# Four graph layers on one core: the scalars' load and copy, and the groups whose degree sums wait for layer 1

## The chip, the core and the metric

The kernel runs on one core of a Trainium2 chip. The metric is the time of one execution in device microseconds (us); the median of three runs of the kernel before is 1097.2 us (1095.84 to 1097.63).

## What is computed

Four graph layers follow each other on x (4096 rows of 64 values) with one dense 4096 x 4096 matrix adj. Each starts from a layer norm with a relu, and adds its result to x:

```python
h = relu(layernorm(x)); x = x + relu((adj @ h) @ W.T + b)                 # layer 0
h = relu(layernorm(x)); x = x + lorentz_attention(h, adj, ...)            # layer 1
h = relu(layernorm(x)); x = x + expmap0(agg(logmap(h), adj / deg) @ W2 + b2)  # layer 2
h = relu(layernorm(x)); x = x + decayed_neighbours(adj != 0) @ (h @ W3) + b3  # layer 3
```

In layer 1, `h` becomes Lorentz vectors hl, q and k; the weights are `adj * sigmoid((2 + 2 q.k) / att_scale + att_bias)`, computed as a sigmoid with a scale `att_a` and a bias `att_b` made of the scalars `att_scale` and `att_bias`, and their sum with hl is normalised. Three more scalars (`scale`, `scale_q`, `scale_k`) enter hl, q and k as exponentials. In layer 2, `deg` is the row sum of adj: it is needed there for the first time, and it is collected while adj passes by in layers 0 and 1.

## The kernel before, in words

**Tiles.** adj is read transposed, four times in all but for half of layer 2. A tile `adj` is 128 partitions x 1024 values (512 KB): two chunks of 128 source rows against 512 target columns. 512 targets are a *block* (`ib`, 0 to 7), two chunks a *group* (`g`, 0 to 15), so a layer has 8 x 16 tiles, each brought by one load on SP's queue (`feed`, line 829). In layers 0 and 1 there are ten tiles of adj (six of pool `adjp`, four of `adj01`): the next load waits until the oldest tile has been used by everyone who needs it.

**Layer 0.** For each tile PE adds two products to a block's sum (`acc<-adj,HA`, `l0_sums`, line 951). Ahead of it stands the layer norm of all x in four parts (`before0`, line 444): DVE takes the mean away, ACT squares, DVE sums, POOL takes the power -0.5, DVE writes `HA`. When a block's 16 groups are summed, a chain follows (`after0`, line 581, then `before1`, line 462): ACT copies the sum to `e`; PE multiplies it with `W0T` and multiplies `dg` with ones to get the degree; DVE adds the bias and writes the block's rows of x; then layer norm, hl, q and k of layer 1 for this *row block*, with DVE, ACT, POOL and PE in turn. At its end stand transposes of q and k on PE and copies to `qT` and `kT` on ACT. Two such chains run at a time.

**Degree sums.** DVE adds the tiles of a block up in `dg` (the first tile is copied, then one addition per tile, then one of the two halves; `degree_sums`, line 925). A tile is not free before both PE and DVE have used it. For each block some groups are left out in layer 0 and added in layer 1 instead, where the same tiles come by again: `FRONT` (line 30) names them for block 0, `LEFT` (3, 7, 11 and 15) for blocks 1 to 6; block 7 leaves none (`group`, line 891).

```python
degree = (g in (LEFT if ib else FRONT) and ib < NB - 1) == (layer == 1)
```

**Layer 1.** `l1` (line 898) is the order of its tiles: block 0's groups 0 to 13, block 1's groups 0 to 13, then groups 14 and 15 of both, then blocks 2 to 7 in order. The first 12 tiles are loaded alternately with the last 12 of layer 0. For blocks 0 and 1 groups are taken in pairs: PE makes the scores (`mm<-qT,kT`, `l1_atts`, line 987), ACT the sigmoids (`sig<-mm`), DVE the products with adj (`sig<-sig,adj`), PE the sums (`acc<-sig,HL`). There is room for the scores of two groups at a time. Group g needs hl and k of row block g // 2, so groups 12 and 13 need row block 6, and pairs are taken strictly in the order of `l1`.

**The scalars.** The five scalars and the biases b0 and b3 are loaded into one row, `line` (seven loads). They stand first in the list `loads`, which `constants` (line 963) issues on ACT's queue from a due time of 18 us on, with the weights W0T, W1T, Wq and Wk behind them. Then PE spreads the row over 128 partitions with one matmul (`tr<-line,ones_row`, due 28 us), and DVE copies the result to `lines`. From it come `es` (ACT), `att_a` and `att_b` (DVE), and the bias in `after0`; the last group of a block in layer 0 is not taken before `lines` is there (line 955).

**What sets the order.** Each piece of work is a generator that yields the engine it needs next and a time from which it may run. `in_turn` (line 758) always takes the piece that can start first, by costs and due times of a small model (`Pace`, line 67), and the instructions are kept in that order on every engine, through one helper (line 139). The profile therefore names line 139 for nearly everything, and work is told apart by its tiles. An engine that waits for its next instruction lets no later one pass.

Of the kernel before, what the change touches and what calls it, by code (L numbers as in the profile page):

```python
# [19 lines left out]
D = 64  # L20
# [6 lines left out]
NG = NC // G  # L27
HALVED = 2
LEFT = (3, 7, 11, 15)
FRONT = (4,5,6,7,)  # L30
LAST = 2
WAIT = 0.6
EARLY = 12
BEHIND = NG - CB // G
# [112 lines left out]
def kernel(ctx: ExitStack, tc: tile.TileContext, a: dict, out: bass.AP):  # L147
# [3 lines left out]
    nc = tc.nc  # L151
    pace = Pace()
    PE, DVE, ACT, POOL = (
        InOrder(tc, e, pace, name)
        for e, name in (
            (nc.tensor, "PE"), (nc.vector, "DVE"), (nc.scalar, "ACT"), (nc.gpsimd, "POOL"),
        )
    )
# [23 lines left out]
    def fetch(t, src, to=loads):  # L182
        to.append(lambda: ACT.dma_start(out=t, in_=src))
# [9 lines left out]
    NS = len(SCALARS)  # L193
    line = const.tile([1, NS + 2 * D], F32, name="line")
    for n, name in enumerate(SCALARS):
        fetch(line[:, n : n + 1], a[name])
    for n, name in enumerate(("b0", "b3")):
        fetch(line[:, NS + n * D : NS + (n + 1) * D], a[name].rearrange("d o -> o d"))
    ones_row = const.tile([1, P], F32, name="ones_row")
    DVE.memset(ones_row, 1.0)  # L200
    lines = const.tile([P, NS + 2 * D], F32, name="lines")
# [58 lines left out]
    def later_constants():  # L260


        def patterns():
            yield "POOL", lambda: 60.0
            for t, one in [(t, 1.0) for t in rbs] + [(t, 0.25) for t in lbs]:
                POOL.memset(t, 0.0)
                for k in (1, 3):
                    POOL.memset(t[:, :, k, 1:2], one)

        def weights_of_ranks():  # L270


            yield "DVE", lambda: 150.0
            near_f = st["rows"].tile([P, P], F32, name="near_f", bufs=1)
            make_lower_triangular(nc, near_f, val=-1.0, diag=False)
            for q in range(4):
                b = slice(q * Q, (q + 1) * Q)
                DVE.tensor_copy(far[b, :], near_f[b, b])
            diag_f = st["rows"].tile([P, P], F32, name="diag_f", bufs=1)
            DVE.tensor_scalar(diag_f, ident, HERE, None, ALU.mult)  # L280
            yield "DVE", lambda: 150.0
            DVE.tensor_add(near_f, near_f, diag_f)
            DVE.tensor_copy(near, near_f)


            yield "DVE", lambda: 150.0
            DVE.memset(pick, 0.0)
            DVE.memset(spread, 0.0)
            for k in range(KH):
                DVE.memset(pick[:, k, k : k + 1], 1.0)  # L290
            for r in range(4):
                yield "DVE", lambda: 150.0
                b = slice(r * Q, (r + 1) * Q)
                for h in range(2):
                    to = spread[b, h, :, h * NC // 2 : (h + 1) * NC // 2]
                    DVE.tensor_copy(
                        to.rearrange("p q (k r) -> p q k r", r=4)[:, :, :, r],
                        ident[b, r * Q : r * Q + KH].unsqueeze(1).to_broadcast([Q, 4, KH]),
                    )

        return patterns(), weights_of_ranks()
# [48 lines left out]
    spare = [0, 1]  # L350

    def bank():
        k = spare.pop(0)
        t = (ps_two if k else ps_tr).tile([P, W], F32, tag=f"tr{k}", name="tr")
        in_use.append((t, k))
        return t

    def emptied(t):
        k = [k for k in in_use if k[0] is t][0]
        in_use.remove(k)  # L360
        spare.append(k[1])
# [219 lines left out]
    def after0(ib, acc, st):  # L581
        e = rows.tile([P, W], F32, tag="e", name="e")
        ACT.copy(e, acc)
        st["acc_free"][ib % 2] = pace.latest
        yield ON_V, lambda: st["dg_done"].get((0, ib))
        dg = st["dg"][0, ib]
        DVE.tensor_add(dg[:, 0, :], dg[:, 0, :], dg[:, 1, :])
        yield TURN

        ps = bank()  # L590
        v, n = ps[:, 0 : CB * D].rearrange("p (c k) -> p c k", k=D), CB * D
        for c in range(CB):
            b = slice(c * P, (c + 1) * P)
            PE.matmul(v[:, c, :], e[:, b], W0T, start=True, stop=True)
            PE.matmul(ps[:, n + c : n + c + 1], dg[:, 0, b], ones_f, start=True, stop=True)
        st["dg_free"][ib % 2] = pace.latest
        yield ON_V
        DVE.tensor_copy(deg[:, cs(ib), :], ps[:, n : n + CB].unsqueeze(2))
        s = rt("h", [P, CB, D])
        DVE.tensor_add(s, v, b0.to_broadcast([P, CB, D]))  # L600
        DVE.scalar_tensor_tensor(
            x[:, cs(ib), :], s, 0.0, x[:, cs(ib), :], ALU.max, ALU.add
        )
        yield ON_V
# [121 lines left out]
    def follow(gen, on=ON_V, evicts=False):  # L726

        tail.append(
            {"gen": gen, "on": on, "at": pace.latest, "slot": None, "evicts": evicts, "need": None}
        )  # L730
# [24 lines left out]
    def latest(*times):  # L755
        return None if None in times else max(times)
# [56 lines left out]
    opened = {}  # L813

    def with_mark(layer, ib, *gens):
        for gen in gens:
            yield from gen
        rows_at[layer, ib] = pace.latest
# [21 lines left out]
    def used(d):  # L840
        d["left"], d["at"] = d["left"] - 1, max(d["at"], pace.latest)

    def ready(t, more=0.0):
        return pace.ready[pace.name(t)] + more

    def arrival(d, more=0.0):
        return ready(d["adj"], more) if "adj" in d else None
# [43 lines left out]
    def group(layer, ib, g):  # L891
        degree = (g in (LEFT if ib else FRONT) and ib < NB - 1) == (layer == 1)
        return {"layer": layer, "ib": ib, "g": g, "degree": degree, "left": 1 + degree, "at": 0.0}
# [1 line left out]


    l0 = [group(0, ib, g) for ib in range(NB) for g in range(NG)]
    l1 = [group(1, ib, g) for ib in range(2) for g in range(BEHIND)]
    l1 += [group(1, ib, g) for ib in range(2) for g in range(BEHIND, NG)]
    l1 += [group(1, ib, g) for ib in range(2, NB) for g in range(NG)]  # L900
    order = l0[: len(l0) - EARLY] + [d for pair in zip(l0[len(l0) - EARLY :], l1) for d in pair]
# [2 lines left out]
    for d in l0 + l1:  # L904
        n = done[d["layer"], d["ib"]] = done.get((d["layer"], d["ib"]), 0) + 1
# [19 lines left out]
    def degree_sums(layer, work):  # L925

        dg = st["dg"]
        for d in work:
            if not d["degree"]:
                continue  # L930
            first = (layer, d["ib"]) not in dg
            yield "DVE", lambda: latest(
                arrival(d, 4.0), st["dg_free"][d["ib"] % 2] if first else 0.0
            )
            if first:
                t = w01.tile([P, G, W], F32, tag="dg", name="dg", bufs=2)
                dg[layer, d["ib"]] = t
                st["dg_free"][d["ib"] % 2] = None
                DVE.tensor_copy(t, d["adj"])
            else:  # L940
                t = dg[layer, d["ib"]]
                DVE.tensor_add(t, t, d["adj"])
            used(d)
            if d is [e for e in work if e["degree"] and e["ib"] == d["ib"]][-1]:
                st["dg_done"][layer, d["ib"]] = pace.latest
# [5 lines left out]
    def l0_sums():  # L951
        for d in l0:
# [6 lines left out]
            if d["last"]:  # L959
                ib = d["ib"]  # L960
                follow(with_mark(1, ib, after0(ib, acc, st), before1(ib, st)), ON_S, evicts=True)

    def constants():
        for k in range(len(loads)):
            yield "ACT", lambda: 18.0 + 0.5 * k
            loads.pop(0)()
        yield "PE", lambda: 28.0 if spare else None
        ps = bank()
        PE.matmul(ps[:, 0 : NS + 2 * D], ones_row, line, start=True, stop=True)
        yield "DVE", lambda: ready(ps)  # L970
        DVE.tensor_copy(lines, ps[:, 0 : NS + 2 * D])
        emptied(ps)
        opened["lines"] = pace.latest
        yield "ACT", lambda: 32.0

        ACT.activation(es, scal[:, 0:3], AF.Exp)

        DVE.reciprocal(att_a, scal[:, 4:5])
        DVE.tensor_scalar(att_a, att_a, 2.0, None, ALU.mult)
        DVE.tensor_add(att_b, att_a, scal[:, 3:4])  # L980
        for k in range(len(later_loads)):
            yield "ACT", lambda: 240.0 + 0.5 * k
            later_loads.pop(0)()
# [543 lines left out]
    def l3_sum():  # L1527
# [33 lines left out]
            (l2_coshs(), 0, once), (l2_clamps_v(), -1, once), (l2_weights2(), 1, lambda d: 2 if d["two"] else 1 if d["first"] else 0),  # L1561
        ),
        l2_clamps(), l2_gathers(), l3_weights(), l3_pass(), l3_masks(), l3_bias(),
        degree_sums(0, l0), degree_sums(1, l1), constants(), *later_constants(),
    ])


# [43 lines left out]
```

## Time and profile before

| what | us |
|---|---|
| median of three runs (lowest, highest) | 1097.2 (1095.84, 1097.63) |
| the profiled execution's own time | 1093.92 |
| its span, first to last instruction | 1092.2 |
| busy: PE, DVE, ACT, POOL | 1038.4, 929.7, 790.0, 260.2 |
| first product of layer 0 / last one | 11.2 / 202.7 |
| chain of layer 0 of blocks 0, 1, 6, 7: first product with W0T | 39.1, 64.4, 169.1, 208.1 |
| q and k of row block 6: transposed on PE | 211.6, 214.1 |
| first 64x512 scores of layer 1 (block 2) | 256.4 |
| mean granted clock of PE | 0.988 of full |

All times are from the span's start. In the views, "x" with a number counts instructions; on PE one matmul of float32 leaves two rows. In brackets behind an instruction stands how long its engine was idle before it and what ended that. In a window's row each engine has its busy time and its instructions; then come PE's granted clock, the busy share of the 16 DMA engines and the GB/s they moved. A row of the timeline has start, duration, engine, operation and tile. Rows of the same kind that follow each other are merged.

### The profile page before, as it was taken

To read this page: it belongs to the slowest core of one execution; us is meant where nothing else is said; L and a number is where in the kernel's file an instruction comes from. 1 tells how busy PE (TensorE), PEld (TensorE's weight loads), DVE (VectorE), ACT (ScalarE), POOL (GpSimd) and SP (SyncE) were. 2 spreads that over 40 slices of the span, in tenths; PEclk is the share of its full clock that TensorE was granted. 3 is DMA by queue.
4 is the path that set the end of the run, shared out by engine and by line. 5 is a ranking of instruction groups with operands and counts; after the bars stand their busy time and mean duration, and the time that the engine had idled before them with its cause. 6 is when DMAs were issued, how large, how long until landed. Compare 5 with 4: busy or idle time off the path is not lost.

```text
span 1092.2 us, 16919 instructions
## 1 busy us (share of the span) xinstructions
PE 1038.4 (95%) x6032; PEld 464.3 (43%) x6032; DVE 929.7 (85%) x1522; ACT 790.0 (72%) x1228; POOL 260.2 (24%) x151
## 2 busy tenths in 40 slices
PE   7989999999999999999999999999999988999998
PEld 3334444333233333354454454444444444454444
DVE  7778999988999999888998999989899999665650
ACT  1144545466777777799989879888798777677776
POOL 3021312110110011243344344334343431000000
PEclk9899999999999999999999999999999999999999
DMA  8999999976687778544553553445536549999950
GB/s 288 405 360 408 398 380 379 310 238 218 208 281 265 240 263 274 171 143 173 181 184 118 179 206 116 174 154 174 174 122 209 191 154 380 376 409 409 410 221 10
DMA packets 76202, 271.77 MB, mean 249 GB/s; under 512 B 9046, under 2 KB 10070, under 8 KB 76118
## 3 DMA queue, kind: packets, MB, share of 16 engines
q1 hardware_dynamic: 75456, 270.57, 68.3%
q8 instruction: 47, 0.77, 0.3%
q14 instruction: 37, 0.30, 0.1%
q10 hardware_dynamic: 662, 0.13, 0.1%
HBM read 269.62 MB, written 1.05 MB: 248 GB/s over the span
## 4 chain that ended last, share of the span: by engine, by line
PE 54%; DVE 21%; issue 8%; ACT 6%; POOL 5%; DMA 4%; SPq 1%; ACTq 0%; DVEq 0%; POOLq 0%
PE acc L139 27%; PE mm L139 17%; PE tr L139 10%; DVE dg L139 5%; POOL v L139 4%; DMA adj<-in_adjT_dram 4%; DVE t L139 4%; DVE w L139 3%; DVE sig L139 3%; ACT sig L139 2%; ACT t L139 1%; ACT lo_sq L139 1%; ACT v L139 1%; DVE h L139 1%; DVE ln_v L139 1%
## 5 line engine op out<-in xcount | busy, mean ns | idle before, releaser
L139 PE MATMUL acc<-w,HA 128*65 128x256 f32 (+1 forms) x736 | 246.2, 470 | 8.6 <-DVE w L139 8.4
L139 POOL TENSOR_SCALAR v<-v 128x1024 f32<-128x1024 f32 (+1 forms) x72 | 171.1, 2376 | 253.3 <-ACT v L139 253.3
L139 ACT ACTIVATE sig<-mm,att_b,att_a 128x1024 f32<-128x1024 f32 x128 | 150.7, 1203 | 57.4 <-PE mm L139 53.5
L139 ACT ACTIVATE wt<-mm,down 128x1024 fp32r<-128x1024 f32 x128 | 136.0, 1110 | 40.0 <-PE mm L139 39.2
L139 DVE TENSOR_TENSOR sig<-sig,adj 128x1024 f32<-128x1024 f32 x128 | 152.7, 1220 | 10.6 <-ACT sig L139 10.4
L139 DVE TENSOR_TENSOR dg<-dg,adj 128x1024 f32<-128x1024 f32 x113 | 137.9, 1221 | 1.6
L139 PE MATMUL mm<-qT,kT 64*64 64x512 f32 (+1 forms) x896 | 130.2, 599 | 6.6 <-ACT sig L139 6.1
L139 PEld LDWEIGHTS acc<-w,HA 128*65 128x65 f32 x736 | 94.2, 138 | 92.0 <-issue 50.1
L139 PE MATMUL acc<-sig,HL 64*64 64x512 f32 (+1 forms) x896 | 130.0, 599 | 1.4 <-DVE sig L139 1.4
L139 PE MATMUL acc<-adj,HA 128*64 128x512 f32 x512 | 125.2, 623 | 5.7 <-DMA adj<-in_adjT_dram 5.4
L139 ACT ACTIVATE v<-v,minus 128x1024 f32<-128x1024 f32 x72 | 79.1, 1098 | 27.4 <-POOL v L139 26.3
L139 DVE SCALAR_TENSOR_TENSOR t<-mm,t 128x1024 f32<-128x1024 f32 x72 | 83.6, 1161 | 14.8 <-PE mm L139 11.0
L139 DVE SCALAR_TENSOR_TENSOR t<-t,v 128x1024 f32<-128x1024 f32 x72 | 83.3, 1157 | 3.4 <-ACT t L139 3.4
L139 DVE TENSOR_TENSOR w<-t,adj 128x1024 f32<-128x1024 f32 x72 | 84.4, 1173 | 1.4
L139 DVE TENSOR_TENSOR w<-tr,adj 128x512 f32<-128x512 f32 x120 | 77.5, 683 | 7.5 <-PE tr L139 7.2
L139 ACT ACTIVATE t<-t 128x1024 f32<-128x1024 f32 x72 | 72.2, 1003 | 12.0 <-DVE t L139 11.9
L139 ACT ACTIVATE v<-mm 128x1024 f32<-128x1024 f32 x72 | 69.6, 967 | 14.0 <-PE mm L139 14.0
L139 PE MATMUL mm<-RT,LT 64*128 64x512 f32 (+1 forms) x288 | 77.9, 618 | 0.0
L139 PE MATMUL acc<-wt,S 128*128 128x512 f32 x256 | 77.1, 426 | 0.6 <-ACT wt L139 0.5
L139 ACT ACTIVATE t<-v 128x1024 f32<-128x1024 f32 x72 | 72.7, 1010 | 2.1
L139 ACT ACTIVATE v<-v 128x1024 f32<-128x1024 f32 x72 | 72.1, 1002 | 0.0
L139 PEld LDWEIGHTS mm<-qT,kT 64*64 64x64 f32 (+1 forms) x896 | 37.8, 140 | 77.8 <-ACT sig L139 36.2
(219 smaller groups left out, 1374.7 us busy)
## 6 DMA issues: line engine op xcount, KB each, us to landing
adj<-in_adjT_dram SPq DMA_DIRECT2D x512, 512.0 KB, 5.4
x<-in_x_dram SPq DMA_DIRECT2D x4, 256.0 KB, 4.6
out_dram<-h SPq DMA_DIRECT2D x8, 128.0 KB, 1.9
W<-in_W_dram ACTq DMA_DIRECT2D x3, 16.0 KB, 3.9
line<-in_b_dram ACTq DMA_DIRECT2D x2, 0.2 KB
W0T<-in_W0T_dram ACTq DMA_DIRECT2D x2, 16.0 KB
line<-in_scale_dram ACTq DMA_DIRECT2D x1, 0.0 KB
line<-in_scale_q_dram ACTq DMA_DIRECT2D x1, 0.0 KB
```

Of the source, the lines that this page charges most:

```text
L139: done = self.tc.keep_in_program_order(getattr(self.engine, op)(*args, **kw))
```

## The change

The seven loads of `line` are no longer put in the list: ACT issues them at once, in front of everything else on its queue. The matmul that spreads them leaves `constants` for a thread of its own with a due time of 10 us in place of 28, and ACT copies the result in place of DVE. `FRONT` is 0 to 3 in place of 4 to 7. And in layer 1 the order of block 0's first 14 groups is 4 to 13 and then 0 to 3, so that the groups that bring degree work stand behind group 13.

```diff
-FRONT = (4,5,6,7,)
+FRONT = (0, 1, 2, 3)
...
     for n, name in enumerate(SCALARS):
-        fetch(line[:, n : n + 1], a[name])
+        nc.scalar.dma_start(out=line[:, n : n + 1], in_=a[name])
     for n, name in enumerate(("b0", "b3")):
-        fetch(line[:, NS + n * D : NS + (n + 1) * D], a[name].rearrange("d o -> o d"))
+        nc.scalar.dma_start(out=line[:, NS + n * D : NS + (n + 1) * D], in_=a[name].rearrange("d o -> o d"))
...
-    l1 = [group(1, ib, g) for ib in range(2) for g in range(BEHIND)]
+    l1 = [
+        group(1, ib, g) for ib in range(2)
+        for g in [g for g in range(BEHIND) if ib or g not in FRONT] + [g for g in FRONT if not ib]
+    ]
...
+    def spread_lines():
+        yield "PE", lambda: 10.0 if spare else None
+        ps = bank()
+        PE.matmul(ps[:, 0 : NS + 2 * D], ones_row, line, start=True, stop=True)
+        yield "ACT", lambda: ready(ps)
+        ACT.copy(lines, ps[:, 0 : NS + 2 * D])
+        emptied(ps)
+        opened["lines"] = pace.latest
+
     def constants():
         for k in range(len(loads)):
             yield "ACT", lambda: 18.0 + 0.5 * k
             loads.pop(0)()
-        yield "PE", lambda: 28.0 if spare else None
-        ps = bank()
-        PE.matmul(ps[:, 0 : NS + 2 * D], ones_row, line, start=True, stop=True)
-        yield "DVE", lambda: ready(ps)
-        DVE.tensor_copy(lines, ps[:, 0 : NS + 2 * D])
-        emptied(ps)
-        opened["lines"] = pace.latest
         yield "ACT", lambda: 32.0
...
-        degree_sums(0, l0), degree_sums(1, l1), constants(), *later_constants(),
+        degree_sums(0, l0), degree_sums(1, l1), spread_lines(), constants(), *later_constants(),
```

## The prediction

> **What bounds the kernel now.** I read the page's busy shares first, then windows of all engines over the first 260 us, then waits and timeline where a window has a hole.
>
> ```profile
> PE 1038.4 (95%) x6032; PEld 464.3 (43%) x6032; DVE 929.7 (85%) x1522; ACT 790.0 (72%) x1228; POOL 260.2 (24%) x151
> ```
>
> PE is busy in 1038 of 1092 us and the change takes no matrix work away, so it can only move PE's idle time. The edits act before 256 us: from the first 64x512 scores of layer 1, block 2 (256.4 us) both instruction orders have given PE the same work, and later they differ only by small swaps (the planner writes each kernel's order when it is built, so both can be read without a run). So I ask how much earlier that point comes. From 220 us to it PE has no gap (20.00 of 20 us in each window); its idle lies before. The first hole, windows of 2 us (span, PE, PEld, DVE, ACT, POOL, clock, DMA share, GB/s):
>
> ```profile
> 16.00:18.00 2.00, 1.69 (x10) 0.40 (x8) 1.51 (x4) 0.43 (x1) 0.50 (x1) 1.00 0.67 266
> 20.00:22.00 2.00, 1.78 (x8) 0.42 (x8) 2.00 (x3) 0.00 (x0) 0.00 (x0) 1.00 0.52 127
> 24.00:26.00 2.00, 0.86 (x6) 0.18 (x4) 1.93 (x3) 0.00 (x0) 0.00 (x0) 0.97 0.76 255
> 28.00:30.00 2.00, 0.76 (x2) 0.32 (x4) 0.00 (x0) 0.00 (x0) 0.00 (x0) 0.50 1.01 389
> 32.00:34.00 2.00, 2.00 (x10) 0.57 (x6) 0.00 (x0) 0.00 (x0) 0.00 (x0) 0.82 1.03 412
> ```
>
> From 30 us on the DMA moves 412 GB/s; in the six windows from 16 to 28 us it moved 266, 242, 127, 280, 255 and 287. The missing 1015 GB/s x 2 us are **4.9 us** of stream. Why, and why DVE then stands still, is in the timeline:
>
> ```profile
> 17.86 0.69 DVE L139 COPY dg<-adj 128x1024 f32<-128x1024 f32 x1
> 18.59 2.48 DVE L139 TENSOR_TENSOR dg<-dg,adj 128x1024 f32<-128x1024 f32 x2
> ...
> 33.68 0.49 PE L139 MATMUL tr<-line,ones_row 1*128 1x133 f32 x2
> ...
> 34.20 0.30 DVE L139 COPY lines<-tr 128x133 f32<-128x133 f32 x1 [6.36 <-PE tr L139]
> ```
>
> The ten tiles of adj are full after groups 0 to 9. PE is done with group 0 at about 11.7 us, but its degree copy runs only at 17.86, and SP's next loads wait for that (up to 4.8 us on DVE's dg). Then DVE stands 6.36 us in front of the scalars' copy: its matmul is queued on PE behind group 14, whose tile comes late through the hole. Meanwhile the clock falls to 0.50.
>
> The second place is the end of layer 0, where DVE is full and PE starts to wait:
>
> ```profile
> 171.80 0.43 DVE L139 SCALAR_TENSOR_TENSOR x<-h,x 128x256 f32<-128x256 f32 x1
> ...
> 209.91 0.41 DVE L139 TENSOR_TENSOR qq<-qkb,lo_s 128x252 f32<-128x252 f32 x1
> ...
> 210.05 0.38 PE L139 MATMUL tr<-ones_f,dg 128*128 128x1 f32 x2 [1.56 <-DVE dg L139]
> ...
> 214.97 1.99 PE L139 MATMUL mm<-qT,kT 64*128 64x512 f32 x8 [0.46 <-ACT kT L139]
> ```
>
> 171.80 is x of row block 6, 209.91 its q of layer 1: 38.1 us. The scores at 214.97 are those of groups 12 and 13, the first that need row block 6.
>
> **Part 1: scalars first, copied by ACT.** Seven DMA issues move ahead of ACT's table load. They took 0.50 + 0.21 + 0.26 + 0.28 + 0.26 + 0.51 = 2.0 us at 15.8 to 19.3. The load (0.78, 1.28 us) then ends near 4.1 us, and ACT's first Square starts at 5.88: hidden by 1.8 us; without that cover 2.0 us. Landing has no row; W's loads took 3.9 us, so the line is in by about 7 us. The matmul now stands behind groups 0 and 1 on PE, at about 12.6 us; its 0.5 us falls where PE waits for adj (0.54 us at 13.67). ACT's copy (DVE's took 0.30) runs at about 13.3 us, between the third Square (12.29) and the fourth (15.80), the only thing queued behind it. DVE loses the copy and the 6.36 us stall. SP's queue holds nothing of this. What I can't see is what seven loads in front of x do to x. All 662 packets of ACT's queue took 0.1% of 16 engines' span, 1.1 us: cost between 0 and 1.1 us, and I take 0, since the line is 7 loads of a few bytes among 19 that include eight of 16 KB.
> [...]
>
> **Part 2: FRONT is 0 to 3.** Groups 0 to 3 are released by PE alone (11.2 to 14.9 us), so loads 10 to 13 go out with no hole, and the tile of group 4 must be free only when load 14 is due. DVE is idle from 17.95 until the fourth HA (POOL's power ends at 19.45), 1.5 us that the old order used. Then copy and adds: 20.2 + 0.7 + 10 x 1.25 = 33.4, three small operations 0.45, the last add 35.1: against 39.75 before, 4.6 us earlier. Block 0's sum of the halves (0.7) follows, PE's degree matmuls (1.72) end at 37.7 against 42.24, and x of block 0 at 38.7 against 44.45: **5.7 us** earlier.
> Some of it goes back. PE reaches those matmuls at 33 us (groups land every 1.31 us at 400 GB/s) and waits about 3 us for DVE. In block 1 the new order puts four adds in a row and then HL straight behind POOL's power (1.9 us), with no add between. By the rows' durations, DVE's adds of block 1 end at 59.9 against 62.17 (2.3 us earlier), x of block 1 at 63.2 against 67.2 (4.0 us). From there to 170 us one block takes 21.0 us, for 16 tiles of 1.31 us: DMA sets the pace, and the lead stays. Its bounds are 2.3 us (DVE's lead) and 7.9 us (the 4.9 us of the first hole and 3 us of a second, 346 GB/s at 60 to 80 us, if that goes too). I take **4.3 us**, near the chain's 4.0 and the DMA's 4.9.
> The clock rows (0.50 at 26 to 32 us, once PE had been mostly idle from 22 us) say that the new 3 us wait may cost speed as well. [...]
>
> **Part 3: groups 0 to 3 behind 13 in layer 1.** Order of block 0: 4 to 13, then 0 to 3. It has a price: groups 12 and 13 need row block 6 and now stand fifth of the seven pairs, so everything behind waits. When row block 6 is ready, PE has given out 6 pairs of scores and 5 of sums before, but 4 and 4 after: 2 x 1.92 + 1.87 (a pair's scores and sums, start to start) = **5.7 us** of PE work moved behind that point. The return: between x and q of row block 6 DVE has 10 products with adj and 17 degree operations before, 8 and 15 after; 4 x 1.14 (two products in a row took 2.27, from 183.05 to 185.32) = **4.6 us** less on an engine without gaps there (39.2 of 40 us in 172 to 212). So q comes 4.3 + 4.6 = 8.9 us earlier, near 201. I follow PE from there: ACT's copy of q 0.41, transposes 0.64 and 0.44, ACT's kT 0.37, so the scores of 12 and 13 run from 2.7 to 4.6 us behind q; the two pairs behind them are held by ACT's two sigmoids (2.30) each and end at 7.0 and 9.4, where sums with finished products stand. Before, PE was full from 219.86, 9.95 behind q: 0.55 us better. Bound of the 4.6 us: 0, if the last tile of layer 0 lands too late, to 4.6; I take 4.6, as DVE and not DMA is full there (278 to 342 GB/s from 180 us). The four degree operations reappear behind group 13: 4.6 us of DVE at a time (220 to 260 us) when it is 74 to 86% busy and PE is the bound: nothing.
>
> **Sum.** 4.3 + 4.6 + 0.55 - 5.7 = **3.8 us** earlier. The profiled execution took 1093.92 us (span 1092.2): 1090.1. It lies 3.3 us under the median of the runs, 1097.2; on that, **1093.4 us**.
>
> **Rivals.**
> - *Larger gain:* the second hole goes as well, lead 7.9 us: 7.9 + 4.6 + 0.55 - 5.7 = 7.4, so 1089.8. For it: fuller buffers. Against: DVE is as late against the stream as before.
> - *No change:* the lead is half eaten by the new waits (POOL's power, degree matmuls): 2.3 + 4.6 + 0.55 - 5.7 = 1.8, or 1095.4. For it: 2.3 us is DVE's own lead, and DVE is the engine that is full later on. FRONT would then mostly swap the wait for the scalars against waits for degree sums and POOL.
> - *Slower, by one mechanism:* row block 6 becomes the gate. PE stands in front of groups 12 and 13 with nothing queued that may pass. The 5.7 us are due whatever comes; they are repaid only if q comes more than 5.1 us earlier. With a lead of 2.3 and DVE's relief lost to late tiles, 2.3 + 0 + 0.55 - 5.7 = -2.8: 1100.0. For it: PE already waits there (1.56 and 0.46 us). Against: DVE's full windows.
>
> **Numbers.** Forecast (gain 2.2 to 5.2) 0.60; larger 0.08; no change 0.17; slower 0.15. A measurement tells about 0.2% (2.2 us) from nothing. Faster 0.68, same 0.17, slower 0.15. The range takes in the bounds of the lead and of DVE's relief: 1089.8 to 1100.0; the forecast's own is 1092.0 to 1095.0.
>
> **What would show it.** Part 1: no wait of DVE's for a copy of lines, ACT's at about 13 us. Part 2: over 380 GB/s in every window of 16 to 30 us; x of block 0 at about 38.7. Part 3: q of row block 6 near 201, scores of 12 and 13 near 204 us, then three pairs of scores together. Wrong if x of block 6 is less than 3 us earlier than 171.8, if PE idles over 5 us in front of groups 12 and 13, or if the 64x512 scores of block 2 don't start near 252.6.

## The result and the profile after

The changed kernel takes 1101.74 us (median of 13 runs, 1097.98 to 1103.67); the kernel before, run beside it, 1095.84 us (13 runs, 1089.83 to 1099.23). The ratio is 1.0054 with an interval of 1.0035 to 1.0073: **slower by 0.5%**, where 0.3% faster was forecast. The profiled execution took 1098.4 us (span 1096.7), one of the fastest of the changed kernel; the one of before took 1093.92 (1092.2). The line of busy times on its page says the same as before did: the same PE work in a longer span.

```profile
PE 1035.8 (94%) x6024; PEld 462.7 (42%) x6024; DVE 929.1 (85%) x1521; ACT 790.8 (72%) x1229; POOL 261.7 (24%) x151
```

**The beginning** went much as forecast, but for a hole that stayed. Windows of 2 us of the changed kernel (columns: span, PE, PEld, DVE, ACT, POOL, clock, DMA share, GB/s):

```profile
16.00:18.00 2.00, 2.00 (x12) 0.63 (x10) 1.27 (x4) 0.63 (x1) 0.44 (x2) 1.00 1.04 416
...
20.00:22.00 2.00, 1.29 (x6) 0.20 (x4) 1.97 (x3) 0.00 (x0) 0.00 (x0) 1.00 0.81 269
...
24.00:26.00 2.00, 0.94 (x4) 0.20 (x4) 1.97 (x2) 0.00 (x0) 0.00 (x0) 1.00 0.94 347
...
28.00:30.00 2.00, 1.68 (x10) 0.26 (x7) 1.97 (x2) 0.00 (x0) 0.00 (x0) 1.00 1.02 414
```

Where 127 GB/s flowed at 20 to 22 us, 269 do now, and from 26 us on the stream is full. A hole is left from 18 to 26 us (340, 269, 299, 347 GB/s; against 412 that is 1.9 us of stream, where 4.9 us were missing). DVE's stall in front of the scalars' copy is gone, since ACT makes the copy (timeline of ACT):

```profile
13.82 0.27 ACT L139 COPY lines<-tr 128x133 f32<-128x133 f32 x1 [0.46 <-PE tr L139]
```

x of block 0, in the kernel before and then in the changed one, is 5.6 us earlier:

```profile
44.03 0.42 DVE L139 SCALAR_TENSOR_TENSOR x<-h,x 128x256 f32<-128x256 f32 x1
```

```profile
38.47 0.42 DVE L139 SCALAR_TENSOR_TENSOR x<-h,x 128x256 f32<-128x256 f32 x1
```

**By row block 6** little of it is left in DVE's chain:

```profile
170.61 0.43 DVE L139 SCALAR_TENSOR_TENSOR x<-h,x 128x256 f32<-128x256 f32 x1
...
205.34 0.41 DVE L139 TENSOR_TENSOR qq<-qkb,lo_s 128x252 f32<-128x252 f32 x1
```

x of row block 6 is 1.2 us earlier (it was at 171.80) and q 4.6 us (209.91). **PE at the gate**, in the timeline of the changed kernel:

```profile
201.25 0.43 PE L139 MATMUL tr<-W0T,e 128*128 128x64 f32 x2
204.34 0.38 PE L139 MATMUL tr<-ones_f,dg 128*128 128x1 f32 x2 [2.66 <-DVE dg L139]
...
207.63 0.69 PE L139 MATMUL tr<-ident,k 128*128 128x128 f32 x2 [0.68 <-ACT qT L139]
208.79 6.22 PE L139 MATMUL mm<-qT,kT 64*128 64x512 f32 x16 [0.46 <-ACT kT L139]
215.28 2.22 PE L139 MATMUL mm<-qT,kT 64*128 64x512 f32 x8 [0.27 <-ACT sig L139]
217.43 1.94 PE L139 MATMUL acc<-sig,HL 128*64 128x512 f32 x8
```

PE first waits 2.66 us for the degree sum of row block 7, which is queued ahead of row block 6's q. Then the scores of groups 12 and 13 and of the next pair run: 16 rows in 6.22 us, where 8 rows took 1.99. The windows show PE's clock there; first the kernel before, then the changed one (columns as above):

```profile
200.00:210.00 10.00, 8.48 (x42) 3.23 (x41) 9.83 (x14) 5.87 (x12) 2.16 (x1) 1.00 0.96 330
210.00:220.00 10.00, 8.77 (x46) 4.09 (x48) 8.23 (x14) 5.09 (x8) 0.78 (x1) 1.00 0.84 276
```

```profile
200.00:210.00 10.00, 6.02 (x34) 3.50 (x31) 9.69 (x18) 1.63 (x4) 1.96 (x1) 0.84 0.56 218
210.00:220.00 10.00, 9.73 (x38) 2.91 (x36) 7.04 (x10) 7.24 (x8) 1.91 (x1) 0.82 0.41 140
```

PE is busy for 15.75 us of the 20 in place of 17.25, and for a third of the 20 us its clock is half (206.7 to 213.5). What half clock does to PE's rows shows in the kernel before, where four rows of layer 0's sums took 1.94 us at 0.50 and four 1.08 at full clock:

```profile
25.82 1.94 PE L139 MATMUL acc<-adj,HA 128*64 128x512 f32 x4 [1.14 <-DMA adj<-in_adjT_dram]
...
38.13 1.08 PE L139 MATMUL acc<-adj,HA 128*64 128x512 f32 x4 [0.19 <-DMA adj<-in_adjT_dram]
```

The stream falls behind as well, to a mean of 179 GB/s from 303 in the two windows: of SP's waits for a free tile there, 13.3 us are for DVE's products with adj, which need the scores. The first degree addition of layer 1's blocks, 261.25 before, comes at 264.61, and the first 64x512 scores of block 2 come 3.35 us later (before, then changed):

```profile
256.40 1.09 PE L139 MATMUL mm<-qT,kT 64*64 64x512 f32 x8
```

```profile
259.75 1.09 PE L139 MATMUL mm<-qT,kT 64*64 64x512 f32 x8
```

To follow a lead through the whole kernel, I paired every instruction of DVE, ACT and POOL with the one that has the same place among those of its operation and tile in before, and took the median difference of their starts in stretches of 25 us of before's time, each named by its beginning (minus: earlier; times from each span's start; one profiled execution each, of kernels that come below):

| kernel | 50 | 100 | 175 | 250 | 425 | 475 | 1000 |
|---|---|---|---|---|---|---|---|
| changed | -4.8 | -5.8 | -4.6 | 3.4 | 3.9 | 5.3 | 4.9 |
| part 1 alone | -5.0 | -2.1 | -1.3 | 1.6 | 0.4 | 5.7 | 6.9 |
| ACT's copy alone | -5.7 | -5.3 | -4.6 | -1.7 | -2.9 | 2.0 | 1.9 |
| part 1, order of before | -3.6 | -3.9 | -4.0 | -3.5 | -3.1 | -3.2 | -3.2 |
| part 2 alone | 0.2 | 0.2 | 0.3 | 1.9 | -2.6 | 7.5 | 8.0 |
| changed, 0 to 3 behind 11 | -3.9 | -2.2 | -1.0 | 0.9 | 1.4 | 1.3 | 2.9 |
| the same, early waits filled | -4.9 | -5.9 | -4.7 | -3.9 | -3.4 | -3.4 | -4.5 |

The changed kernel loses 8.0 us between 175 and 250 us, at the gate, and 1.5 more where layer 2 begins (there the clock was 0.62 in its window of 472 to 476 us).

### The profile page after: what moved, and what is told of

It reads as the page before. It is cut to its first block, busy times and chain, and to the rows that moved or that the text cites. A ratio compares the mean times of both kernels' runs of the same rounds, so it can differ in the third digit from the quotient of the medians.

```text
span 1096.7 us, 16904 instructions
## 1 busy us (share of the span) xinstructions
PE 1035.8 (94%) x6024; PEld 462.7 (42%) x6024; DVE 929.1 (85%) x1521; ACT 790.8 (72%) x1229; POOL 261.7 (24%) x151
## 4 chain that ended last, share of the span: by engine, by line
PE 54%; DVE 22%; ACT 7%; issue 7%; POOL 5%; DMA 3%; ACTq 0%; SPq 0%; POOLq 0%; DVEq 0%
PE acc L139 26%; PE mm L139 18%; PE tr L139 11%; DVE dg L139 6%; POOL v L139 4%; DVE t L139 3%; DVE w L139 3%; DMA adj<-in_adjT_dram 2%; DVE sig L139 2%; ACT sig L139 2%; ACT t L139 1%; ACT v L139 1%; DVE ln_v L139 1%; DVE h L139 1%; POOL lo_s L139 1%
## 5 line engine op out<-in xcount | busy, mean ns | idle before, releaser
L139 PE MATMUL acc<-adj,HA 128*64 128x512 f32 x512 | 120.6, 602 | 6.2 <-DMA adj<-in_adjT_dram 5.8
L139 ACT ACTIVATE t<-t 128x1024 f32<-128x1024 f32 x72 | 72.2, 1003 | 12.2 <-DVE t L139 12.1
```

The costliest lines, as they stand in the source:

```text
L139: done = self.tc.keep_in_program_order(getattr(self.engine, op)(*args, **kw))
```

## The experiments

At the start stood theory G: the gate of row block 6 eats the gain, and parts 1 and 2 bring what was forecast. Its rival was L: the lead of parts 1 and 2 is lost on the way, whatever layer 1's order. Ratios are to runs of the kernel before on the same chip; medians of before lay between 1094.36 and 1096.18 us in the six sets of runs.

| kernel | median us (runs) | ratio | interval |
|---|---|---|---|
| changed | 1101.74 (13) | 1.0054 | 1.0035 to 1.0073 |
| scal | 1099.62 (12) | 1.0052 | 1.0033 to 1.0071 |
| order | 1109.08 (6) | 1.0135 | 1.0102 to 1.0168 |
| scal_front | 1102.48 (6) | 1.0074 | 1.0049 to 1.0099 |
| gate_open | 1096.45 (12) | 1.0014 | 0.9993 to 1.0036 |
| loads_first | 1092.56 (12) | 0.9982 | 0.9963 to 1.0000 |
| scal_held | 1090.85 (12) | 0.9974 | 0.9958 to 0.9991 |
| act_copy | 1098.53 (12) | 1.0038 | 1.0018 to 1.0059 |
| warm | 1098.03 (12) | 1.0032 | 1.0014 to 1.0050 |
| front_only | 1100.25 (12) | 1.0050 | 1.0028 to 1.0072 |
| behind11 | 1092.71 (12) | 0.9977 | 0.9956 to 0.9998 |
| front_behind11 | 1094.37 (12) | 0.9999 | 0.9979 to 1.0020 |
| all_held | 1097.97 (12) | 1.0028 | 1.0011 to 1.0046 |
| gate_warm | 1099.30 (12) | 1.0028 | 1.0010 to 1.0046 |
| behind11_warm | 1089.71 (9) | 0.9956 | 0.9933 to 0.9980 |
| held_behind11 | 1091.83 (12) | 0.9962 | 0.9943 to 0.9980 |
| gate_warm7 | 1097.45 (12) | 1.0022 | 1.0006 to 1.0039 |
| held_behind11_warm | 1091.08 (12) | 0.9969 | 0.9953 to 0.9985 |

### The parts, and the gate opened

**scal**, part 1 alone: the change without its new FRONT and without its new order of layer 1.

```diff
-FRONT = (0, 1, 2, 3)
+FRONT = (4,5,6,7,)
...
-        for g in [g for g in range(BEHIND) if ib or g not in FRONT] + [g for g in FRONT if not ib]
...
+    l1 = [group(1, ib, g) for ib in range(2) for g in range(BEHIND)]
```

> Part 1 alone: the seven scalar loads come first, the spreading matmul is due at 10 us, ACT copies; FRONT stays 4 to 7 and layer 1 keeps its order. Theory G (the gate: the changed kernel loses its time where groups 12 and 13 wait for row block 6, and the early edits gain): DVE has no wait of 6.4 us for the copy any more, x of block 0 comes 2 to 5 us earlier than 44.0 us, and the time is 1 to 3 us under the kernel before. Rival L (the early edits cost: scalars in front of x, tiles released in another order): x's first part lands later, the lead is gone by block 6, and the time is 1 to 4 us over before.

Measured: 1.0052, as slow as the whole change, although x of block 0 comes at 37.53, 6.5 us earlier than before. This tells against G alone: something in part 1 loses more than it brings.

**order**, part 3 alone, on the kernel before:

```diff
-    l1 = [group(1, ib, g) for ib in range(2) for g in range(BEHIND)]
+    l1 = [group(1, 0, g) for g in (4,5,6,7,8,9,10,11,12,13,0,1,2,3)] + [group(1, 1, g) for g in range(BEHIND)]
```

> Part 3's order alone: block 0 of layer 1 goes 4 to 13, then 0 to 3, with FRONT still 4 to 7 and the old scalars; the degree work then stands first in layer 1, as before. Theory G: the gate has its price with nothing to repay it: scores of groups 12 and 13 in fifth place, PE idle behind the last sum of layer 0 by 4 us or more, and 5 to 9 us over before. Rival L: the order costs little by itself, 0 to 2 us over before.

Measured: 1.0135, 14.8 us, above what either theory allowed. Without FRONT's relief the new order is dear; why by so much is not shown.

**scal_front**, parts 1 and 2, with layer 1 in its old order.

> Parts 1 and 2 without part 3: scalars first, FRONT 0 to 3, layer 1 in its old order 0 to 13, so the four degree operations stand first in layer 1. Theory G: the lead at block 0 (5.6 us) shrinks to that of the DMA stream (2.1 us) and stays; no gate, so 0.5 to 3 us under before. Rival L: 3 to 6 us over before, like the changed kernel.

Measured: 1.0074, 8.1 us, above the range of L too. Taking part 3 away from the change does not help. With FRONT 0 to 3, groups 0 to 3 then bring their degree sums back first in layer 1. It is row block 7 that comes late: x to q of row block 6 took only 31.8 us, but x of row block 7 came at 223.85, against 207.66 in the changed kernel. That the degree sums hold it up is argued, not shown.

**gate_open**, the changed kernel in which groups 12 and 13 of block 0 in layer 1 read k and hl of groups 10 and 11, so that they wait for row block 5 and not 6; their own k and hl are left out of that block's sums.

```diff
+        src = g - 2 if layer == 1 and ib == 0 and g in (12, 13) else g
...
-                            d["ps"][to, c, :], st["kT"][half, d["g"], to],
+                            d["ps"][to, c, :], st["kT"][half, d["src"], to],
```

> The changed kernel, but groups 12 and 13 of block 0 in layer 1 read k and hl of groups 10 and 11 (row block 5) in place of row block 6, so that nothing in front of row block 6's end waits for it; it leaves out these groups' own k and hl, the work is the same. Theory G: the scores of these groups come before the q of row block 6, PE's idle time in 196 to 212 us falls from 4 us to under 2, and the time is 5 to 8 us under the changed kernel, so 0 to 3 us under before. Rival L: no more than 2 us under the changed kernel.

Measured: 1.0014. The gate is worth 0.4% (4.4 us by the ratios, whose intervals just touch), and with it open the change still gains nothing. So both G and L hold in part.

### Why part 1 alone is slower

Three theories were left for it: A, the seven loads ahead of x hold the first HA back; B, the planner, whose model sees an earlier start, gives the chains of all later blocks another order, and that order is worse; C, PE's new waits in block 0's chain halve its clock.

**loads_first**: only the loads move to the front. No other instruction changes its place.

```diff
-        fetch(line[:, n : n + 1], a[name])
+        nc.scalar.dma_start(out=line[:, n : n + 1], in_=a[name])
```

> The kernel before with one edit: the seven loads of the scalars' row are issued first on ACT; matmul and DVE's copy stay where they were, and all other instructions keep their order. Theory A (loads ahead of x hold x and so the first HA back): slower than before by 1 to 4 us, 1096 to 1099. Theory B (part 1's loss, 4.7 us in the run with part 1 alone, comes from the new order that the planner gives to the chains of later blocks): no difference, within 1 us of before. Theory C (it comes from PE's new waits in block 0's chain and the half clock behind them): no difference either, since DVE's stall of 6.36 us stays; the half clock of 26 to 32 us stays too.

Measured: 0.9982 (0.9963 to 1.0000). No loss: A falls. x of block 0 even comes at 41.55, 2.5 us earlier.

**scal_held**: part 1, while the planner's model is told of the old way, so that everything else keeps the order of before. The loads, the matmul (behind group 1) and ACT's copy are issued outside the plan; in `constants` only the model's times advance.

```diff
+            if d is l0[1]:
...
+                tc.keep_in_program_order(
+                    nc.tensor.matmul(ps[:, 0 : NS + 2 * D], ones_row, line, start=True, stop=True)
+                )
+                tc.keep_in_program_order(nc.scalar.copy(lines, ps[:, 0 : NS + 2 * D]))
...
-        PE.matmul(ps[:, 0 : NS + 2 * D], ones_row, line, start=True, stop=True)
+        pace.issue("PE", "matmul", (ps[:, 0 : NS + 2 * D], ones_row, line), dict(start=True, stop=True))
```

> Part 1 (seven loads first, matmul of the row behind group 1, copy by ACT) with every other instruction of every engine in the order of before. Theory A: slower than before, as part 1 alone was (1098 to 1100). Theory B (planner's new order costs): faster than before, by the 4.9 us of the first hole at most and 1 us at least: 1090 to 1094. Theory C (PE's waits and the half clock at 55 to 62 us): the lead of x of block 0 is 5 to 6.5 us and is gone by block 2, and the time is that of before or slower, 1095 to 1099.

Measured: 0.9974 (0.9958 to 0.9991), faster than before, at the lower edge of B's range. The same edit is 0.78% apart by its order alone (8.5 us), with intervals that don't meet: B is shown for this edit. How much of the 8.5 us the new order costs through PE's clock is not separated. In the table of leads it is the flattest row: 3.6 to 4.0 us to 200 us, 3.2 at the end.

**act_copy**: only the copy goes to ACT; loads and matmul keep their due times. PE's order is then that of scal but for the place of the row's matmul, and differs from that of before all the way from the first chain on.

```diff
-        yield "DVE", lambda: ready(ps)
-        DVE.tensor_copy(lines, ps[:, 0 : NS + 2 * D])
+        yield "ACT", lambda: ready(ps)
+        ACT.copy(lines, ps[:, 0 : NS + 2 * D])
```

> The kernel before with one edit: the copy of the scalars' row is ACT's in place of DVE's; loads and matmul keep their due times, so nothing goes ahead of x. DVE's stall of 6.36 us goes, and the planner orders the later blocks anew, much as with part 1 alone. Theory A: no loss (1090 to 1095). Theory B: as slow as part 1 alone, 1098 to 1100. Theory C: between, 1095 to 1099.

Measured: 1.0038, B's side again, with nothing ahead of x. Its profiled execution had full clock to 1091 us, so its losses are those of the order alone. They lie in two places: the lead falls from 4.6 to 1.7 us around the end of layer 0, and goes from 2.9 us early to 2.0 us late where layer 1 passes into layer 2. Windows there, first of scal_held, then of act_copy:

```profile
480.00:484.00 4.00, 3.57 (x17) 1.24 (x16) 4.00 (x7) 3.17 (x5) 3.79 (x2) 1.00 0.44 131
484.00:488.00 4.00, 4.00 (x25) 2.68 (x24) 3.76 (x14) 3.96 (x4) 0.76 (x1) 1.00 0.00 1
```

```profile
480.00:484.00 4.00, 2.54 (x21) 2.14 (x20) 3.64 (x7) 2.98 (x4) 2.27 (x2) 1.00 0.00 0
484.00:488.00 4.00, 2.60 (x8) 0.57 (x6) 3.32 (x4) 2.29 (x3) 3.40 (x2) 1.00 0.46 131
```

PE is busy for 5.1 of 8 us where it was for 7.6, and DVE and ACT have pauses too. The two show the same stretch of time, not the same work; over the whole passage, 420 to 540 us, PE is idle for 7.6 us in act_copy and 4.6 in scal_held. From 470 to 496 us PE's waits are for DVE's tiles w and t (4.2 us). So no engine is full there, and the pieces of layer 2 wait for each other in the order that was laid down for them. This is some 450 us behind the edit.

**warm**: the changed kernel with 16 products that nobody reads, where PE waits in block 0's chain. The rest keeps its order.

```diff
+    def keep_clock(ps, n):
+        for _ in range(n):
+            tc.keep_in_program_order(nc.tensor.matmul(ps[:, 0:P], ident, ident, start=True, stop=True))
...
-        yield from transposed(hl, D, hlT[0:D, :])
+        yield from transposed(hl, D, hlT[0:D, :], 8 if ib == 0 else 0)
```

> The changed kernel with 16 more products of 128x128 on PE that nobody reads, all in block 0's chain: 4 ahead of its degree matmuls, 4 ahead of the transposes of h, 8 ahead of those of HL, where PE stood 0.96, 1.2 and 2.1 us in the profiled execution. All other instructions keep their order. Theory C (the half clock at 55 to 62 us, which the runs of part 1 and of the open gate show and the profiled execution of the changed kernel does not, eats the lead): faster than the changed kernel (1101.7) by 2 to 5 us, 1096.5 to 1099.5, with no half clock before 200 us. Theories A and B: no difference, 1100.5 to 1102.5, or slower by at most the 4.5 us of the added products.

Measured: 1.0032 against 1.0054 for the changed kernel. That is 2.4 us in C's direction, in C's range by the median, but the intervals overlap. Its profile has full clock from 30.7 to 204.8 us, but so has that of the changed kernel. What it is about shows in gate_open, whose order is that of the changed kernel up to there. Windows of 3.4 us of gate_open, then of the changed kernel with the same wait in the first of them:

```profile
54.20:57.60 3.40, 1.25 (x8) 0.56 (x8) 2.06 (x5) 0.46 (x3) 1.01 (x1) 0.96 1.01 407
57.60:61.00 3.40, 3.40 (x14) 1.83 (x10) 3.30 (x5) 0.82 (x2) 0.00 (x0) 0.50 0.73 233
61.00:64.40 3.40, 3.40 (x10) 0.74 (x9) 0.46 (x1) 3.15 (x15) 0.00 (x0) 0.54 0.87 290
```

```profile
51.50:54.90 3.40, 1.27 (x10) 0.36 (x4) 1.47 (x5) 0.68 (x4) 1.01 (x1) 1.00 1.03 410
54.90:58.30 3.40, 3.40 (x20) 1.65 (x20) 3.30 (x4) 2.16 (x5) 0.00 (x0) 1.00 1.02 401
```

Behind the wait for HL (2.15 us) one execution runs at half clock for 6.8 us, behind the same wait (2.13 us) the other not at all. x of block 1 comes at 66.89 in the first and 61.51 in the second; 1.0 us of that was there at x of block 0. In the runs of the changed kernel the time goes with the clock: those with a mean clock of 0.993 and 0.994 took 1098.0 to 1098.4 us, those with 0.984 and 0.985 took 1102.2 to 1103.7. Why the clock fell behind one of the two waits and not behind the other is not shown.

### What the gate costs

**front_only**, part 2 alone:

```diff
-FRONT = (4,5,6,7,)
+FRONT = (0, 1, 2, 3)
```

> Part 2 alone: FRONT is 0 to 3, layer 1 keeps its order (0 to 13 in block 0), the scalars' row comes as before (loads from 18 us, copy by DVE). It leaves the stall of 6.36 us in front of DVE's copy. The prediction's theory: earlier tiles give a lead of 2.3 to 4.3 us that stays: 1090 to 1093. Theory B (the planner gives the chains of later blocks another order, which costs 3 to 8 us, as part 1 alone with and without its new order showed): 1096 to 1101.

Measured: 1.0050, B's range. Up to 200 us it runs as before did, 0.3 us later, so FRONT by itself brings no lead at all; at the passage to layer 2 it goes from -2.6 to +7.5.

**behind11**, the changed kernel with groups 0 to 3 between 11 and 12:

```diff
+    l1 = [group(1, 0, g) for g in (4,5,6,7,8,9,10,11,0,1,2,3,12,13)] + [group(1, 1, g) for g in range(BEHIND)]
```

> The changed kernel with groups 0 to 3 of block 0 in layer 1 between 11 and 12, not behind 13: groups 12 and 13 are the last pair again, and their row block 6 holds nothing up; DVE's four degree sums come back between x and q of row block 6. Gate theory: the 5.3 us that the open gate gave, less what DVE's four sums take (4.6 at most): 1096.5 to 1101. Theory B alone (only the plan of the later blocks costs): no difference from the changed kernel, 1100.5 to 1102.5, as the orders differ only around the gate.

Measured: 0.9977 (0.9956 to 0.9998), faster than before and 3.8 us below the lower end of what G allowed: moving the four groups in front of 12 is worth 0.77% (8.4 us by the ratios). B alone, which saw no difference, is out too: by operations and tiles the two orders differ only between 198 and 242 us, so no other plan of later blocks has a part in this. PE's windows show it, beside those of the changed kernel above:

```profile
200.00:210.00 10.00, 9.55 (x46) 3.62 (x42) 9.76 (x13) 6.04 (x12) 2.49 (x1) 1.00 0.78 311
210.00:220.00 10.00, 9.46 (x51) 4.19 (x50) 9.69 (x17) 4.92 (x7) 1.91 (x1) 1.00 0.57 213
```

19.0 us of PE in place of 15.75, and full clock. q of row block 6 is later here, at 210.03 (DVE has the four sums back), and it does not stop PE, which has two more pairs to give out until then. The first two rows are the scores of those pairs, the last those of groups 12 and 13:

```profile
205.05 1.99 PE L139 MATMUL mm<-qT,kT 64*128 64x512 f32 x8
207.48 2.22 PE L139 MATMUL mm<-qT,kT 64*128 64x512 f32 x8 [0.45 <-ACT sig L139]
...
212.32 1.94 PE L139 MATMUL acc<-sig,HL 128*64 128x512 f32 x8
...
216.42 1.99 PE L139 MATMUL mm<-qT,kT 64*128 64x512 f32 x8
```

gate_open gave less, 4.4 us, though its groups 12 and 13 waited for nothing: in its trace the four sums on DVE behind group 13 let row block 7 come late (PE waits 0.76 us for its HL at 231 us), and its clock was half for 3.4 us at 211. That this is the whole difference is argued, not shown.

**front_behind11**, the same without part 1:

> Parts 2 and 3 without part 1, with groups 0 to 3 placed between 11 and 12. Gate theory: without the gate, FRONT's earlier tiles remain: 1091 to 1096. Theory B: the plan of the later blocks is new again and costs 3 to 8 us: 1097 to 1102.

Measured: 0.9999. FRONT 0 to 3 with its groups in a good place changes nothing measurable against 4 to 7. The 1097 to 1102 us of theory B are missed: a new plan is not always a worse one.

**all_held**, the whole change in the order that the planner gives to parts 2 and 3 without part 1 (the device of scal_held):

> All of the change, but the planner is told that the scalars' row comes by the old way (loads from 18 us, matmul from 28 us, copy on DVE), while it really comes first and by ACT: the order is that which the planner gives to parts 2 and 3 without part 1. It differs from the order of the changed kernel in few places. Theory B as far as part 1's model goes: faster than the changed kernel by up to 4 us if those few places matter, 1097.5 to 1100; the same, 1100.5 to 1102.5, if parts 2 and 3 bring the new order of the later blocks by themselves.

Measured: 1.0028 against 1.0054 for the changed kernel, in the range of an effect by the median, but the intervals overlap. Its order differs from that of the changed kernel in few places, and the gate is in it.

**gate_warm** and **gate_warm7**: warm with products at the gate too, to take the half clock out of its price. The first put its ten in front of row block 6's degree matmuls; the wait there is row block 7's, so the 2.66 us and the half clock stayed. The second has them where the wait is; both have two more ahead of the transposes of k.

```diff
-        keep_clock(ps, 4 if ib == 0 else 0)
+        keep_clock(ps, 4 if ib == 0 else 10 if ib == 7 else 0)
```

> The run with 16 products in block 0's chain, with 12 more where PE stands at the gate: 10 ahead of the degree matmuls of row block 6 (2.66 us of idle) and 2 ahead of the transposes of its k (0.68). If the half clock behind that wait (10.2 us long in the last profile, the scores of groups 12 and 13 at 6.22 us in place of 4.0) is a good part of the gate's price: 2 to 4 us faster than with the 16 alone (1098.0), 1094 to 1096.5. If the price is only the order (PE has nothing else to give out, whatever its clock): no difference, 1097 to 1099.

> As gate_warm, with the 10 products ahead of the degree matmuls of row block 7 in place of 6: the wait of 2.66 us at the gate is that of block 7's degree sum, which stands on PE in front of row block 6's q, and gate_warm left it and the half clock (206.1 to 212.9) as they were, so it tested nothing. If the half clock at the gate is a good part of its price: 2 to 4 us faster than with the 16 products alone (1098.0), 1094 to 1096.5, with scores of 12 and 13 at about 4.0 us for two groups' pairs. If the price is the order: 1097 to 1099, with full clock there.

Measured: 1.0028 and 1.0022, no difference from warm (1.0032). In gate_warm7 the wait is filled (0.43 us of it is left) and the clock still falls:

```profile
203.30:206.70 3.40, 2.79 (x22) 2.20 (x20) 3.40 (x5) 0.41 (x1) 0.28 (x1) 0.94 0.82 274
206.70:210.10 3.40, 2.26 (x9) 1.75 (x10) 2.90 (x7) 0.96 (x2) 0.00 (x0) 0.50 0.04 14
```

So the half clock was not taken out, and how the 8.4 us divide into order and clock stays open. The trace bounds one part: of the 16 rows at 6.22 us, 2.2 us at most are the clock's (two pairs at 1.99 each would be 4.0). In the kernel before, at full clock, the same two pairs took 4.96 us (214.97 to 219.93), since the second waits for ACT's sigmoids; by that only 1.3 us are.

**behind11_warm**, **held_behind11** and **held_behind11_warm**: behind11 with warm's 16 products, with part 1 outside the plan, and with both.

> Groups 0 to 3 between 11 and 12 (1092.7) with the 16 products of 128x128 in block 0's chain. If the half clock at 55 to 62 us still eats the lead there (its profile has 3.4 + 3.4 + 6.8 us of half clock before 64 us), 2 to 4 us faster: 1088.5 to 1091. If only the gate matters, 1092 to 1094.

> Groups 0 to 3 between 11 and 12, the scalars' row first and by ACT, and the planner told of the old way, so that the order is that of parts 2 and 3 without part 1 (front_behind11, 1094.4). What it gains on that run is part 1 by itself in that order: 2 to 4 us as between the kernel before and the run that held its order, 1090.5 to 1092.5; none, 1094 to 1095, if FRONT has already taken what part 1 could give.

> All that helped, together: scalars' row first in the order planned for the old way, FRONT 0 to 3 behind 11, 16 products in block 0's chain. If the half clock of the early waits costs here as it did with behind11 (3.0 us): 1088 to 1090. If the held order has no half clock at 55 to 62 us to lose (its profile shows none): 1091 to 1092.5, no difference from held_behind11.

Measured: 0.9956 (0.9933 to 0.9980), 0.9962 (0.9943 to 0.9980) and 0.9969 (0.9953 to 0.9985). All three beat both kernels, and are not told apart from each other. The 16 products gained 2.3 us on behind11 and lost 0.8 on held_behind11, so the price of the early half clock is not settled by them. Part 1 outside the plan is worth 0.37% here (front_behind11 against held_behind11, intervals that just touch), 0.26% on the kernel before.

## Why the prediction was wrong, step by step

**"From 256.4 us on ... later they differ only by small swaps."** It failed as a rule. The changed kernel happened to lose only 1.5 to 2 us behind that point, but act_copy, scal and front_only lost 5 to 10 us at the passage into layer 2. Listing two orders side by side shows that the work is the same, not that it takes the same time.

**Part 1** was right in itself. ACT's copy ran at 13.82 (forecast 13.3), the loads ahead of x cost nothing that loads_first could tell, and with the order of before part 1 brought 2.9 us by the ratio. Hidden they were not quite: the last two were issued at 4.50, and ACT's first Square began at 6.33 in place of 5.88.

**Part 2, "loads 10 to 13 go out with no hole".** This step failed. Load 10 went out at 19.07, against 20.09 before, though groups 0 and 1 were through PE at 13.37. SP's waits in the first 30 us, in the kernel before and then in the changed one (total, times, longest):

```profile
SPq L837 <- DMA adj<-in_adjT_dram: 15.3, 7, 4.8
SPq L837 <- DVE dg L139: 0.4, 1, 0.4
```

```profile
SPq L837 <- DMA adj<-in_adjT_dram: 10.2, 3, 6.1
SPq L837 <- DVE dg L139: 5.5, 7, 0.9
```

By the profile SP waited there for earlier loads to land, before and after; the 4.8 us on DVE's dg that the prediction names lie at 31 to 36 us, where DVE stands in front of the scalars' copy. FRONT was not what filled the stream: over the first 30 us it is 296 GB/s before, 303 in front_only, 325 in loads_first, where only the seven loads move, and 327 in the changed kernel. x of block 0 agrees: 44.03 before, 44.36 in front_only, 37.53 with part 1 alone and 38.47 with both. Why the place of the seven loads matters so much is not shown.

**Part 2's lead, 4.3 us "and the lead stays".** x of block 0 ended at 38.89 (forecast 38.7) and x of block 1 at 61.9 (63.2): these numbers held, but by part 1, and PE's wait for the degree sum of block 0 was 0.96 us, not 3. At x of row block 6 the lead was 1.2 us, outside the bounds of 2.3 to 7.9. The stream does not account for it: windows from the start, of the kernel before and then of the changed one, have it ahead by 2.2 us at 150 us (at 412 GB/s), by nothing at 180 and by 3.9 us at 200.

```profile
0.00:150.00 150.00, 133.97 (x677) 60.04 (x678) 121.99 (x187) 56.20 (x203) 36.04 (x45) 0.95 0.97 375
0.00:180.00 180.00, 162.95 (x830) 72.83 (x832) 151.17 (x253) 70.38 (x266) 43.00 (x50) 0.96 0.97 376
0.00:200.00 200.00, 182.22 (x920) 79.96 (x921) 170.67 (x277) 81.74 (x283) 46.79 (x51) 0.97 0.97 370
```

```profile
0.00:150.00 150.00, 132.26 (x694) 60.33 (x696) 124.01 (x191) 55.76 (x200) 35.31 (x45) 1.00 0.98 381
0.00:180.00 180.00, 160.57 (x840) 72.25 (x841) 153.25 (x256) 73.47 (x271) 45.14 (x50) 1.00 0.97 376
0.00:200.00 200.00, 179.47 (x930) 79.30 (x932) 172.00 (x277) 83.94 (x291) 47.07 (x51) 1.00 0.97 378
```

The loss goes with the order: x of block 0 to x of block 6 took 132.1 us in the new one (in behind11_warm as well), 127.8 in the old one, and 127.4 in scal_held, which has the old order with the early start and is 3.6 to 4.0 us ahead at every x of blocks 0 to 6. Which wait of the new order takes it is not shown.

**Part 3's relief, 4.6 us:** 3.4 by the profiles (x to q 34.7 against 38.1). Together q came 4.6 us earlier, not 8.9; the prediction's own point for the rival was 5.1.

**PE full 9.4 us behind q:** 12.1. The scores of 12 and 13 began 3.45 us behind q in place of 2.7, and the three pairs took 8.7 us in place of 6.7, 16 of their 24 rows mostly at half clock. The chance of speed lost in a new wait was named for block 0's wait, and is in no term of the sum; in the profiled execution the clock stayed full there and was half at the gate.

**The sum** closes with what was measured: 1.2 + 3.4 - 2.15 (12.1 against 9.95) - 5.7 = -3.25; the first degree addition of layer 1 came 3.4 us later. So the terms, with 5.7 us for the moved work, account for the loss up to there, and the rival "slower, by one mechanism" was the case: row block 6 is the gate. That its -2.8 lies so near is luck: it had 2.3 and 0 for lead and relief where 1.2 and 3.4 were measured, and the slower catch-up behind q, which it left out, made up for that. The 1.5 us where layer 2 begins come on top. The median lies 5.9 us above before's, further than the profiles (4.5): the profiled execution of the changed kernel, with the best clock of its runs (0.994), was 3.3 us under their median, that of before 1.9 us under its own.

**Four sums behind group 13, "nothing":** q of row block 7 came 33.2 us behind its x in the changed kernel and 28.5 before. PE has other work there, so what they cost is not shown by itself.

## What to carry to other kernels

When a planner writes the order of the instructions, an edit is two changes: what it does, and the new order of everything behind it. Run the edit with the old order held before you believe or discard it; here the same edit was 0.5% slower or 0.3% faster by that alone, while another new order cost nothing. And work that needs a late result should stand last in an order that lets nothing pass (here PE stood 2.66 us in front of one degree sum): count what the engine still has to give out when the result comes, before counting how much earlier it may come.

## What the runs showed of the hardware

The granted clock of PE fell to half for stretches of 3.4 us (473.0 to 476.4 in the changed kernel), 6.8 us (206.7 to 213.5 there) or 10.2 us (at the gate in warm, from 204.8 on). Where it did so differs between executions of the same order: from 10 to 198 us, where the orders of the changed kernel, gate_open and behind11 are the same, it fell nowhere in the first, at 36.8 and 57.3 us in the second, and at 25.1, 38.7 and 55.8 us in the third. The changed kernel's runs, 5.7 us apart at the ends, go mostly with their mean clock. Behind a wait of 2.1 us it was half in one execution and full in another. And it fell in gate_warm7 behind a stretch in which PE was busy for 2.79 of 3.40 us, nearly all of it small products (128x64 and 128x1) and transposes: filling a wait did not keep the clock there. The lengths are multiples of 3.4 us; what sets the half clock off no run here shows.
